# Moving half a chunk of gates ahead of the main loop, and reordering the last three chunks, in a fused recurrence and feed-forward kernel

## The chip, the cores and the metric

The kernel runs on one core of one Trainium2 chip. The metric is the device time of one execution in microseconds (us). The engines are PE (TensorE, with its weight loads listed apart as PEld), DVE (VectorE), ACT (ScalarE), POOL (GpSimd) and SP (SyncE, which here issues nearly all DMAs).

## The reference

Two residual layers with a layer norm behind each. The first is a gated recurrence over 4096 positions of two sequences, the second a feed-forward layer with binarized weights.

```python
u = x @ W_in + b_in                       # 256 -> 64
g = sigmoid(x @ W_gate + b_gate)          # 256 -> 256
h_t = tanh(h_prev @ A + u_t @ Bm)         # one step of the recurrence
y_t = h_t @ C.T + u_t @ D.T
y_t = g_t * y_t + (1 - g_t) * x_t
x1 = layernorm(x + (ys @ W_out + b_out + x))
bw1, bw2 = alpha1 * sign(w1), alpha2 * sign(w2)
h = gelu(x1 @ bw1.T + b1)                 # 256 -> 1024
out = layernorm(x1 + h @ bw2.T + b2)
```

## The kernel before

The 4096 positions of each sequence are cut into 64 segments of 64, which run side by side, so that a recurrence step is one product of 128 x 128 states (two sequences by 64 segments). Each segment but the first starts from a guess: 48 warm-up steps over the last 48 positions come before the 64 real ones, 112 steps in all. At the end a comparison (`compare`, `count`) tells whether the guesses held; a slow path, which does not run here, stands behind it.

The rest of the work is cut into 16 chunks of 512 tokens: 4 recurrence steps times 128 columns. A chunk c goes through these parts:

- gates (`gates`, L313 on PE, tanh on ACT at L365): two halves m, each of two k products, each cut into four quarters of 128 columns. The generator takes up to `size` quarters at a time between yields. Its PSUM tiles come from the pool p_1, three buffers with the tag "h", shared with the up products.
- `mix` (L374 on PE, L381 on DVE, a row added on POOL at L359) and `mix_end` (L386 and L389 on DVE).
- `project` (L399 on PE, L410 on DVE), `stats1` (L255 to L264 on DVE, a power on POOL at L265), `shift` (L270 on DVE), `norm` (L278 on ACT, or L280 on DVE).
- a transposition of the normed chunk: `turn` does it on PE (L430), splits it on ACT (L438) and DVE (L440) and serves chunks 0, 1 and 15; `blocks` does it with a DVE transpose (L449) and sixteen DMAs on SP (L455), followed by `split_hi` (L463 on ACT) and `split_lo` (L467 on DVE), for the chunks between.
- `rest` adds a bias row on POOL (L359).
- `up` in four groups (L486 on PE, eight matmuls of 512 columns; gelu at L496 and a cast at L505 on ACT), `low` (L512 on DVE), and `down` in four groups (sixteen matmuls, L528 on PE).
- `scale` (L544) and `add` (L550) on DVE, `stats`, and `store`, which norms on ACT (L278) and writes the output (L565).

The order of all instructions is written out by hand, and each engine works through its own in that order. A function `emit` counts an assumed PE time of every piece (`COST`), and issues one recurrence step (`steps`: L157 on PE, then tanh on ACT at L158) each time the count passes `pace`. Before the loop the gates of chunks 4 to 7, 0 to 3, 8 and 9 run as small parts of three quarters between the steps (`parts`). In the loop the count is switched off, each iteration c has four places for a step, and the steps run out after iteration 10. The iteration interleaves up of chunk c, down of chunks c-1 and c, mix and project of chunk c+2 and the transposition of chunk c+1. The gates of chunks 10 to 15 come at half a chunk per iteration, from a second generator:

```python
early = gates([ch[i] for i in (4, 5, 6, 7, 0, 1, 2, 3, 8, 9)], 3)
...
late = gates(ch[10:], TB)
```

Tiles are taken from pools with a fixed number of buffers: eight for x transposed ("xt"), nine for the gates ("tg"), one each for the PSUM tags "m" (mix, project, turn) and "o" (down). DMAs wait in the order of SP's queue.

Of the kernel before, what the change touches and what calls it, by code (L numbers as in the profile page):

```python
# [18 lines left out]
KD = DM // P  # L19
# [7 lines left out]
NC = L // SPC  # L27
TB = N // P
# [9 lines left out]
def gated_recurrence_then_binary_ffn(  # L38
# [16 lines left out]
    nc = tc.nc  # L55
# [235 lines left out]
    def later(what, *args):  # L291
        if waiting is None:
            what(*args)
        else:
            waiting.append((what, args))
            if len(waiting) > 1 and not held:
                what, args = waiting.pop(0)
                what(*args)

    def gates(chunks, size, x_of=lambda c: x_tiles[c.c]):  # L300

        room = size
        for c in chunks:
            xt_ = x_of(c)
            c.t = wk.tile([P, KD, N], FP, tag="tg", name=f"tg{c.nm}", bufs=TGB)
            for m in range(KD):
                ps = p_1.tile([P, N], FP, tag="h", name=f"ps_g{c.nm}_{m}")
                for k in range(KD):
                    i = 0
                    while i < TB:  # L310
                        n = min(room, TB - i)
                        cut = bass.ds(i * P, n * P)
                        nc.tensor.matmul(  # L313
                            ps[:, cut],
                            w_gate[:, k, bass.ts(m, P)],
                            xt_[:, k, cut],
                            start=k == 0 and i == 0,
                            stop=k == KD - 1,
                            skip_group_check=True,
                        )  # L320
                        i += n
                        room -= n
                        if k == KD - 1 and i == TB:
                            later(c.tanh, m, ps)
                        if room == 0:
                            room = size
                            yield

    class Chunk:

# [28 lines left out]
                nc.gpsimd.tensor_tensor(r[:, i, :], r[:, i, :], row, ALU.add)  # L359

        def gate(self):
            yield from gates([self], TB, lambda c: c.xt)

        def tanh(self, m, ps):
            nc.scalar.activation(  # L365
# [193 lines left out]
        def store(self, blocks=range(TB), engine=nc.vector, queue=nc.sync):  # L559

            cut = slice(blocks[0], blocks[-1] + 1)
            if engine is nc.scalar:
                self.st2.shift(blocks)
            self.st2.apply(blocks, engine)
            queue.dma_start(  # L565
                out=self.at(out, self.c)[:, cut, :], in_=self.x1[:, cut, :]
            )
            yield
# [13 lines left out]
        def down_end(self):  # L582
# [28 lines left out]
            add(3)  # L611
            st2.shift([0, 1])
            store(0, nc.scalar)
            store(1, nc.scalar)
            st2.gather([2, 3])
            st2.merge([2, 3])
            st2.root([2, 3])
            store(2, nc.vector)
            store(3, nc.vector)
            yield  # L620
# [17 lines left out]
    ch = [Chunk(c, f"{c}") for c in range(NC)]  # L638
# [8 lines left out]
    def ready():  # L647
        return done < len(plan) and plan[done] // SPC in have_u

    def next_steps():  # L650
        nonlocal done
        steps(plan[done])
        done += 1
        if done == WARM:
            first_states()
        for i in range(3):
            if done == WARM + (i + 1) * SPC:
                ch[i].load_h()
        if waiting and not held:
            for what, args in waiting:  # L660
                what(*args)
            waiting.clear()

    def emit(what, pieces, pace=5600):
        nonlocal since
        for _ in pieces:
            since += COST.get(what, 0)
            if since >= pace:
                since = min(since - pace, pace // 2)
                if ready():  # L670
                    next_steps()

    def step():
        if ready():
            next_steps()

    def do(i, what, *args, pace=5600):
        if not 0 <= i < len(ch):
            return
        if what == "load":  # L680
            need = WARM + (ch[i].c + 1) * SPC
            while done < need:
                next_steps()
            ch[i].load_u()
            ch[i].load_h()
        elif what in ("load_n", "load_x", "load_gate_x"):
            getattr(ch[i], what)()
        else:
            emit(what, getattr(ch[i], what)(*args), pace)

    early = gates([ch[i] for i in (4, 5, 6, 7, 0, 1, 2, 3, 8, 9)], 3)

    def parts(n, pace):
        emit("part", (next(early, None) for _ in range(n)), pace)

    ET = mybir.EngineType
    with tc.manual_schedule(engines={ET.PE, ET.Activation, ET.DVE, ET.Pool, ET.SP}):
# [39 lines left out]
        for i in range(4):  # L737
            ch[i].xt = x_tiles[i]
        ch[0].in_x = ch[1].in_x = True
        parts(1, 600)  # L740
        do(0, "mix", pace=850)
        do(0, "mix_end")
# [13 lines left out]
        do(0, "norm")  # L756
        do(1, "project", 1, pace=1700)
        do(1, "stats1")
        parts(1, 1700)
        while waiting:  # L760
            next_steps()
        waiting = None
# [4 lines left out]
        do(1, "norm", nc.vector)  # L767
        do(0, "rest")
        next(mixed)
        parts(2, 1700)  # L770
        for i in (4, 5):
            do(i, "load_x")
        end = len(ch) - 1
        parts_met = compare()
        since = -1 << 40
        late = gates(ch[10:], TB)
        for c in range(end):
            far = 0 < c < end - 1
            if far:
                do(c + 1, "shift")  # L780
                do(c + 1, "norm")
                do(c - 1, "low", 3)
                do(c + 1, "blocks")
            do(c, "up", 0)
            if c == end - 1:
                do(c - 1, "low", 3)
                do(c + 1, "shift")
                do(c + 1, "norm")
            step()
            do(c - 1, "down", 2)  # L790
            if c > 0:
                do(c + 2, "mix")
            do(c, "low", 0)
            mixed = ch[c + 2].mix_end() if 0 < c < end - 1 else iter(())
            next(mixed, None)
            if c == end - 1:
                assert done == len(plan), done
                next(parts_met)
                next(parts_met)
            do(c + 3, "load")  # L800
            do(c + 6, "load_x")
            if c % 2 == 0:
                do(10 + c // 2, "load_gate_x")
            do(c, "up", 1)
            step()
            do(c - 1, "down", 3)
            next(mixed, None)

            if c <= 12 or c == end - 1:
                do(c - 1, "add")  # L810
            if c <= 12:
                do(c - 1, "stats")
            if 1 <= c <= 12:
                emit("gate", (next(late, None) for _ in range(KD)))
            if not far:
                do(c + 1, "turn")
            do(c, "low", 1)
            if c == end - 2:
                do(c - 1, "add")
            if c > 12:  # L820
                do(c - 1, "stats")
            if c == end - 1:
                next(parts_met)
                next(parts_met)
            do(c + 1, "rest")
            do(c, "up", 2)
            step()
            if far:
                do(c + 1, "split_hi")
            do(c, "low", 2)  # L830
            if c < end - 1:
                do(c - 1, "store", range(TB), nc.scalar)
            do(c + 3, "load_n")
            do(c, "down", 0)
            do(c + 2, "project", 0)
            if c == end - 2:
                do(c + 1, "split_lo")
            do(c + 2, "project", 1)
            if far and c < end - 2:
                do(c + 1, "split_lo")  # L840
            do(c + 2, "stats1")
            do(c, "up", 3)
            if c == end - 1:
                do(c - 1, "store", range(TB), nc.scalar)
            step()
            do(c, "down", 1)
# [82 lines left out]
```

## Time and profile before

| what | value |
|---|---|
| time, median of 3 runs | 437.67 us (437.33 to 437.82) |
| the profiled execution: its own time, its span | 437.67 us, 435.9 us |
| granted TensorE clock, mean | 0.994 |
| instructions | 6818 |
| matmuls of the gates, L313 | 208, busy 66.2 us |
| matmuls of the recurrence, L157 | 224, busy 43.8 us |
| up products, L486 | 512, busy 92.9 us (hi) and 80.1 us (lo) |
| row additions on POOL, L359 | 128, busy 107.6 us |

The span runs from the first to the last instruction of the core; the execution's own time is 1.8 us longer. Busy time is summed by engine. A matmul's row covers its fill and its drain, so that neighbouring rows overlap, and the start of one row after another says how fast PE goes. In a row of the timeline the brackets give the idle time of the engine before it and what ended it. The first 8 us wait for the first loads; from 8 to 86 us PE works on u, gates and steps; the loop runs from 86 to about 408 us; what follows is the last chunk, whose end (from 427 us) is DVE, ACT, POOL and the last stores.

### The profile page before, as it was taken

The page shows a single profiled execution, that of the slowest core. Times are in us where ns is not written, and L with a number is a line of the kernel's source. Part 1 is how long each engine was busy: PE and PEld are TensorE (multiplying, and loading weights), DVE is VectorE, ACT ScalarE, POOL GpSimd, SP SyncE. Part 2 cuts the span into 40 slices and gives each one's busy share as a digit, 9 for nine tenths or more (in the row PEclk, how much of TensorE's full clock was granted, in tenths as well). Part 3 has the DMA queues.
Part 4 walks back from the last instruction along what each step waited for, and adds up shares of the span by engine and source line. Part 5 has one row for each costly group of instructions (what it writes and reads, how often), then busy time and mean ns, then how long its engine had stood idle before and what let it go on. Part 6 is the DMA issues. An engine that isn't in the chain of part 4 may idle for free.

```text
span 435.9 us, 6818 instructions
## 1 busy us (share of the span) xinstructions
PE 425.5 (98%) x2402; PEld 344.3 (79%) x2402; DVE 332.4 (76%) x569; ACT 286.0 (66%) x480; POOL 155.8 (36%) x176
## 2 busy tenths in 40 slices
PE   8999999999999999999999999999999999999992
PEld 5665767788888879797979797978888888888982
DVE  0245937895979798888888897979797979797674
ACT  2443452486587776767677776777767585849881
POOL 1000050474143435253525443444343444533413
PEclk9999999999999999999999999999999999999997
DMA  8877713400251615152426242534233232311102
GB/s 297 300 282 261 269 36 128 163 2 0 44 174 44 217 46 178 38 186 80 144 66 192 76 144 69 166 102 124 91 107 109 58 111 60 111 36 50 48 2 102
DMA packets 31479, 51.34 MB, mean 118 GB/s; under 512 B 5328, under 2 KB 19664, under 8 KB 31440
## 3 DMA queue, kind: packets, MB, share of 16 engines
q1 hardware_dynamic: 30864, 50.48, 36.4%
q8 instruction: 21, 0.34, 0.3%
q10 hardware_dynamic: 576, 0.37, 0.3%
q14 instruction: 18, 0.15, 0.1%
HBM read 31.43 MB, written 8.39 MB: 91 GB/s over the span
## 4 chain that ended last, share of the span: by engine, by line
PE 89%; DVE 5%; ACT 2%; DMA 1%; issue 1%; POOL 1%; SPq 0%; POOLq 0%; DVEq 0%
PE ps_h L486 25%; PE ps_o L528 25%; PE ps_g L313 12%; PE ps_z L399 11%; PE ps_y L374 6%; PE ps_s L157 6%; PE ps_u L131 3%; DMA xt<-in_xT 1%; DVE hlo L512 1%; ACT xn L278 1%; POOL rs_b L265 1%; PE ps_t L430 1%; DVE bs_b L255 1%; DVE d L381 1%; ACT h L496 1%
## 5 line engine op out<-in xcount | busy, mean ns | idle before, releaser
L528 PE MATMUL ps_o<-sg,hhi 128*128 128x256 f32 x496 | 121.4, 286 | 0.0
L528 PE MATMUL ps_o<-sg,hlo 128*128 128x256 f32 x496 | 117.9, 279 | 0.1
L496 ACT ACTIVATE h<-ps_h,bias_c,al 128x512 f32<-128x512 f32 x128 | 95.5, 771 | 16.8 <-PE ps_h L486 13.0
L528 PEld LDWEIGHTS ps_o<-sg,hhi 128*128 128x128 f32 x496 | 93.5, 189 | 1.1 <-DVE o L544 0.3
L528 PEld LDWEIGHTS ps_o<-sg,hlo 128*128 128x128 f32 x496 | 93.5, 188 | 1.1 <-DVE hlo L512 0.3
L486 PE MATMUL ps_h<-xhi,sg 128*128 128x512 f32 x256 | 92.9, 444 | 0.3 <-ACT h L496 0.3
L359 POOL TENSOR_TENSOR xn<-xn,bo_r 128x256 f32<-128x256 f32 x64 | 54.7, 888 | 88.6 <-DMA xn<-in_x 78.4
L512 DVE TENSOR_TENSOR hlo<-h,hhi 128x1024 fp32r<-128x1024 f32 (+1 forms) x65 | 79.5, 1240 | 5.0 <-ACT hhi L505 5.0
L486 PE MATMUL ps_h<-xlo,sg 128*128 128x512 f32 x256 | 80.1, 394 | 0.2
L265 POOL TENSOR_TENSOR rs_b<-rs_b,neg_half 128x4 f32<-128x4 f32 (+1 forms) x17 | 28.1, 1655 | 115.1 <-DVE rs_b L264 105.0
L505 ACT CAST hhi<-h 128x1024 fp32r<-128x1024 f32 (+1 forms) x65 | 67.4, 1039 | 2.0
L313 PE MATMUL ps_g<-xt,w_gate 128*128 128x384 f32 (+3 forms) x208 | 66.2, 430 | 0.1
L486 PEld LDWEIGHTS ps_h<-xhi,sg 128*128 128x128 f32 x256 | 46.5, 189 | 18.9 <-issue 11.7
L158 ACT ACTIVATE st<-ps_s 64x128 f32<-64x128 f32 x112 | 30.0, 268 | 45.7 <-PE ps_s L157 45.3
L486 PEld LDWEIGHTS ps_h<-xlo,sg 128*128 128x128 f32 x256 | 48.0, 188 | 11.9 <-DVE xlo L440 0.7
L157 PEld LDWEIGHTS ps_s<-st,wab 128*128 128x128 f32 x224 | 38.5, 189 | 21.6 <-ACT st L158 9.7
L359 POOL TENSOR_TENSOR xn<-xn,b_r 128x256 f32<-128x256 f32 x64 | 52.9, 855 | 1.1 <-PE ps_t L430 1.1
L399 PE MATMUL ps_z<-w_out,tg 128*128 128x256 f32 x224 | 50.6, 379 | 0.0
L399 PEld LDWEIGHTS ps_z<-w_out,tg 128*128 128x128 f32 x224 | 41.4, 190 | 5.1
L157 PE MATMUL ps_s<-st,wab 128*128 128x128 f32 x224 | 43.8, 277 | 0.1
L278 ACT ACTIVATE xn<-xn,nm_a,rs_a 128x256 f32<-128x256 f32 x60 | 31.2, 591 | 14.4 <-DVE nm_a L270 14.3
L265 POOL TENSOR_TENSOR rs_a<-rs_a,neg_half 128x4 f32<-128x4 f32 x16 | 17.2, 1072 | 65.0 <-DVE rs_a L264 63.0
(79 smaller groups left out, 481.5 us busy)
## 6 DMA issues: line engine op xcount, KB each, us to landing
xt<-in_xT SPq DMA_DIRECT2D x35, 512.0 KB, 4.4
xn<-in_x SPq DMA_DIRECT2D x16, 512.0 KB, 3.4
out_y<-xn SPq DMA_DIRECT2D x15, 512.0 KB, 2.6
xlo<-xb SPq DMA_DIRECT2D x208, 32.0 KB, 1.9
hu<-st SPq DMA_DIRECT2D x32, 128.0 KB, 2.3
w1t<-in_w1T SPq DMA_DIRECT2D x2, 512.0 KB, 4.9
w1n<-in_w SPq DMA_DIRECT2D x2, 512.0 KB, 6.1
w2t<-in_w2T SPq DMA_DIRECT2D x2, 512.0 KB, 5.2
```

The lines of the kernel that those rows point to most:

```text
L157: nc.tensor.matmul(p_h, ab, st[:, j].rearrange("p b k -> p (b k)"), start=True, stop=True)
L158: nc.scalar.activation(h_of[:, j + 1].rearrange("p b k -> p (b k)"), p_h[TOP, :], AF.Tanh)
L265: nc.gpsimd.tensor_tensor(rs, rs, neg_half[:, cut], ALU.pow)
L278: nc.scalar.activation(r, r, AF.Identity, bias=self.sh[:, i : i + 1], scale=rs)
L313: nc.tensor.matmul(ps[:, cut], w_gate[:, k, bass.ts(m, P)], xt_[:, k, cut], start=k == 0 and i == 0, stop=k == KD - 1, skip_group_check=True,)
L359: nc.gpsimd.tensor_tensor(r[:, i, :], r[:, i, :], row, ALU.add)
L399: nc.tensor.matmul(self.ps_z[:, i, :], self.y[:, k, bass.ts(i, P)], w_out[:, k, :], start=k == 0, stop=k == KD - 1,)
L486: nc.tensor.matmul(ps, sg1[:, k, bass.ts(j, P)], part[:, k, :], start=n == 0, stop=n == 2 * KD - 1,)
L496: nc.scalar.activation(to, ps.rearrange("p (a i c) -> p a i c", a=P // 32, c=32) if self.far else ps, AF.Gelu, bias=b1_c[:, j : j + 1], sc ...
L505: nc.scalar.copy(hi[:, part, :], h[:, part, :])
L512: nc.vector.tensor_sub(lo[:, i, :], h[:, i, :], hi[:, i, :].bitcast(FP))
L528: nc.tensor.matmul(ps[:, i, :], part[:, j % 2, bass.ts(tb, P)], sg2[:, j, :], start=j == 0 and part is self.h[j // 2][0] and first, stop=j ...
```

## The change

- One generator `stream` now serves all gates. Its piece size is a list of one number that is changed from 3 quarters to 4 before the loop. Two more parts are taken before the loop, one before `turn` of chunk 0 and one at the loop's entrance: with them half of chunk 10's gates (one m of two) is done there. The load of chunk 10's x for the gates moves ahead of chunk 0's mix; in the loop the gates begin with iteration 2.
- The step that stood behind the first up group of an iteration now stands behind the first down group (chunk c-1's third). Iteration 0, which has no such down group, issues no step there.
- In iteration 13, `rest` of chunk 14 and the store of chunk 12 move behind project and stats1 of chunk 15, the store behind the last up group. The store's shift on DVE is taken out of it and put behind `split_lo` of chunk 14; `store` skips the shift where it has been done.
- In iteration 14, `turn` and `rest` of chunk 15 move from before to behind the third up group of chunk 14.

No arithmetic is added or removed.

```diff
     def gates(chunks, size, x_of=lambda c: x_tiles[c.c]):
 
-        room = size
+        room = size[0]
...
                         if room == 0:
-                            room = size
                             yield
+                            room = size[0]
...
-            if engine is nc.scalar:
+            if engine is nc.scalar and not hasattr(self.st2, "sh"):
                 self.st2.shift(blocks)
...
-    early = gates([ch[i] for i in (4, 5, 6, 7, 0, 1, 2, 3, 8, 9)], 3)
+    size = [3]
+    stream = gates([ch[i] for i in (4, 5, 6, 7, 0, 1, 2, 3, 8, 9, *range(10, NC))], size)
...
+        do(10, "load_gate_x")
         parts(1, 600)
         do(0, "mix", pace=850)
...
         do(1, "stats1")
-        parts(1, 1700)
+        parts(2, 1700)
         while waiting:
             next_steps()
...
         next(mixed)
-        parts(2, 1700)
+        parts(3, 1700)
...
-        late = gates(ch[10:], TB)
+        size[0] = TB
...
-            step()
             do(c - 1, "down", 2)
+            if c > 0:
+                step()
             if c > 0:
                 do(c + 2, "mix")
...
-            if c % 2 == 0:
+            if c > 0 and c % 2 == 0:
                 do(10 + c // 2, "load_gate_x")
...
-            if 1 <= c <= 12:
-                emit("gate", (next(late, None) for _ in range(KD)))
-            if not far:
+            if 2 <= c <= 12:
+                emit("gate", (next(stream) for _ in range(KD)))
+            if c == 0:
                 do(c + 1, "turn")
...
-            do(c + 1, "rest")
+            if c < end - 2:
+                do(c + 1, "rest")
             do(c, "up", 2)
+            if c == end - 1:
+                do(c + 1, "turn")
+                do(c + 1, "rest")
             step()
...
-            if c < end - 1:
+            if c < end - 2:
                 do(c - 1, "store", range(TB), nc.scalar)
...
             if c == end - 2:
                 do(c + 1, "split_lo")
+                ch[c - 1].st2.shift(range(TB))
             do(c + 2, "project", 1)
...
             do(c + 2, "stats1")
+            if c == end - 2:
+                do(c + 1, "rest")
             do(c, "up", 3)
-            if c == end - 1:
+            if c >= end - 2:
                 do(c - 1, "store", range(TB), nc.scalar)
```

More of the change, by code (lines that the diff above doesn't have):

```diff
@@ L361, in gate @@
         def gate(self):
-            yield from gates([self], TB, lambda c: c.xt)
+            yield from gates([self], [TB], lambda c: c.xt)
         def tanh(self, m, ps):
@@ L689, in do @@
             emit(what, getattr(ch[i], what)(*args), pace)
-    early = gates([ch[i] for i in (4, 5, 6, 7, 0, 1, 2, 3, 8, 9)], 3)
+    size = [3]
+    stream = gates([ch[i] for i in (4, 5, 6, 7, 0, 1, 2, 3, 8, 9, *range(10, NC))], size)
     def parts(n, pace):
-        emit("part", (next(early, None) for _ in range(n)), pace)
+        emit("part", (next(stream) for _ in range(n)), pace)
     ET = mybir.EngineType
```

## The prediction

> **What bounds the kernel now.** I read the page first, then the windows by stage, then the chain of waits in order of time, then the timeline of each engine around the places where the chain leaves PE.
>
> ```profile
> PE 425.5 (98%) x2402; PEld 344.3 (79%) x2402; DVE 332.4 (76%) x569; ACT 286.0 (66%) x480; POOL 155.8 (36%) x176
> ...
> PE 89%; DVE 5%; ACT 2%; DMA 1%; issue 1%; POOL 1%; SPq 0%; POOLq 0%; DVEq 0%
> ```
>
> PE is the bound, and no other engine is near it. But a PE row includes its pipelined end, so 98% busy hides short stalls. The windows (PE busy first after the length) say where to look:
>
> ```profile
> 82.00:94.00 12.00, 11.67 (x62) 8.87 (x60) 11.24 (x20) 10.09 (x18) 8.85 (x10) 1.00 0.13 47
> 94.00:380.00 286.00, 286.00 (x1626) 239.54 (x1625) 238.93 (x404) 207.62 (x323) 118.86 (x128) 1.00 0.35 104
> 380.00:410.00 30.00, 29.65 (x185) 25.85 (x184) 26.58 (x51) 22.85 (x31) 10.43 (x9) 1.00 0.12 34
> ```
>
> From 94 to 380 us PE never stops, at granted clock 1.00: there, only moving work to or from PE counts. Gaps lie at the loop's entrance and in chunks 13 and 14. PE's timeline shows them:
>
> ```profile
> 83.25 0.52 PE L430 MATMUL ps_t<-ident,xn 128*128 128x128 f32 x3
> 83.93 0.77 PE L430 MATMUL ps_t<-ident,xn 128*128 128x128 f32 x5 [0.17 <-ACT xn L278]
> 84.53 0.60 PE L239 MATMUL ps_al<-al,ones 128*128 128x256 f32 x2
> ...
> 85.98 0.70 PE L486 MATMUL ps_h<-xhi,sg 128*128 128x512 f32 x2
> 86.59 1.10 PE L486 MATMUL ps_h<-xlo,sg 128*128 128x512 f32 x2
> ...
> 90.74 0.49 PE L157 MATMUL ps_s<-st,wab 128*128 128x128 f32 x2
> ...
> 391.85 0.62 PE L486 MATMUL ps_h<-xhi,sg 128*128 128x512 f32 x2
> 392.54 0.74 PE L486 MATMUL ps_h<-xlo,sg 128*128 128x512 f32 x2
> 393.57 0.73 PE L486 MATMUL ps_h<-xhi,sg 128*128 128x512 f32 x2 [0.28 <-ACT h L496]
> ```
>
> Compare starts, not durations. Chunk 0's turn takes 1.28 us from 83.25 to 84.53, where chunk 1's takes 0.80 to 0.87 (91.06 to 91.86). Chunk 14's first up group takes 2.75 us (391.85 to the first down product at 394.60), where the chain gives 1.83 for eight such matmuls. ACT and DVE tell why chunk 14 is late:
>
> ```profile
> 389.21 1.05 ACT L463 CAST xhi<-xlo 128x1024 fp32r<-128x1024 f32 x1 [4.48 <-DVE hlo L512]
> 390.77 2.08 ACT L278 ACTIVATE xn<-xn,nm_b,rs_b 128x256 f32<-128x256 f32 x4 [0.51 <-DVE nm_b L270]
> 392.75 1.43 ACT L496 ACTIVATE h<-ps_h,bias_c,al 128x512 f32<-128x512 f32 x2
> ...
> 390.03 0.70 DVE L270 SCALAR_TENSOR_TENSOR nm_b<-mv_b,rs_b 128x4 f32<-128x4 f32 x1 [0.91 <-POOL rs_b L265]
> 390.78 1.71 DVE L467 TENSOR_TENSOR xlo<-xlo,xhi 128x1024 fp32r<-128x1024 f32 x1
> ```
>
> ACT puts chunk 12's store (L278) ahead of the last gelus of chunk 13 (L496), whose PSUM tile up(14,0) needs; DVE puts that store's shift, which waits for POOL's power, ahead of split_lo(14) (L467).
>
> **The change part by part.** The sum is made against the profiled execution, 437.67 us for a span of 435.9; 437.67 is also the median of the runs shown.
>
> **1. Half of chunk 10's gates before the loop.** Counting room by quarters (128 columns, 0.645 us per three, so 0.215 each): 54 parts covered 160 quarters, 56 parts cover 168. Eight quarters, 1.72 us, enter before the loop; chunk 1 loses two 512-column pairs, also 1.72 (112.93 to 114.65 in the chain). PE's total is unchanged; what can change is stalls. Before, from step 67 (82.38) to down(0,0) (93.92) is 11.54 us. Content: 5 steps at 0.22 (1.10), 7 quarters (1.51), two turns at 0.87 (1.74), mean_w2 0.44, three up groups at 1.83 (5.49): 10.28. Stalls: 1.26. With the change, the same content plus 1.72:
> - Part 53 and step 68 now come before turn(0), and reach it at 84.1. The wait for the norm ending at 83.88 is covered, but step 68 itself wants to start at 83.89 and needs step 67's tanh, which ACT does behind the norm and ends at 84.04: new stall 0.2.
> - Three parts and step 69 after mean_w2 put up(0,0) at 87.8 instead of 85.98. Its low halves (DVE L440) end at 87.13: that wait goes, and so does the one of the step at 90.74, now issued early.
> - ACT starts chunk 0's gelus 1.1 us later, so step 71 (wants 94.29) meets step 70's tanh (about 94.26): 0.05, up to 0.2.
> Down(0,0) comes at 82.38 + 12.0 + 0.25 = 94.6, 0.7 later than before; chunk 1 gives 1.72 back. Gross gain 1.0.
>
> The extra tanh of chunk 10 (0.67 us) moves on ACT from 114.69 to about 88, between hi(0) and the first gelu, which PE doesn't offer before 88.7: nothing. Its load of 512 KB (4.4 us) moves on SP ahead of chunk 1's states; its buffer was free once the u of chunks 13 to 15 or chunk 8's gates were done (64 us), and SP issues nothing between 63.7 and 67.25: nothing. If SP did wait for longer, chunk 1's states (issued 67.25, landed 69.76) would hold mix(1), at 70.67, by all beyond 0.9 us.
>
> **What covers chunk 1 then?** The price is here: the half of the gates also hid the block transposes of chunk 2.
>
> ```profile
> 121.45 1.05 ACT L463 CAST xhi<-xlo 128x1024 fp32r<-128x1024 f32 x1 [2.89 <-DMA xlo<-xb]
> 122.40 2.08 ACT L278 ACTIVATE xn<-xn,nm_b,rs_b 128x256 f32<-128x256 f32 x4
> 124.39 1.42 ACT L496 ACTIVATE h<-ps_h,bias_c,al 128x512 f32<-128x512 f32 x2
> ```
>
> The sixteen DMAs land at 121.4 whatever PE does. up(2,0) moves from 125.90 to 124.18: hi is ready at 122.5, lo (DVE L467) at about 123.8 and wanted at 124.64, but its second half wants at 125.1 the PSUM tile that the gelu starting at 124.39 frees at 125.2 (the same pair freed PE 0.82 after its start at 393.57). New stall 0.1, and about 0.1 more where the next step meets ACT. Net of part 1: 0.8.
>
> **2. The step behind the first down run.** The step keeps its two 109 ns matmuls and its 0.27 us tanh. Without the move, chunk 2's step would stand at 126.1 and wait for the tanh at 126.79 to 127.05; moved, it stands at 127.9. That saves 0.9 us that part 1 would otherwise cost, and nothing against before. On ACT the tanh stays behind the cast, which ends 2 us after the moved step: no blocking. The trace has no step between a down run and a mix; its four places cost 0.28 (the moved one), 0.15, 0.18 and 0.21 us, as differences of the chain between iterations 5 and 11, the one with steps and the other without. Ten steps move, so the new place may give 0.1 each or take 0.03. Part of the 0.28 is a slower pace of down matmuls (117 against 113 ns each), which no step sets, so I take 0 and keep -1.0 to +0.3 in all.
>
> **3. Chunk 13's order.** split_lo(14) can follow split_hi (ends 390.26): done at 391.5, not 392.5. up(14,0)'s lo is wanted at 392.3: 0.24 gone. The gelus of up(13,3) start at 390.2 instead of 392.75, freeing their tile at 391.0, wanted at 392.77: the rest of the 0.92 gone. The store then runs 392.6 to 394.7 and gelu(14,0) ends at 396.0 against 396.6: no new wait. rest(14) (four POOL adds, 3.80 us) now starts after POOL's power for chunk 15, near 396.8. Here a rule speaks against the change: with it beside split_lo, L467 took 1.71 us, beside none 1.23 (123.17): 0.48 per instruction. The Trainium skill, "SBUF — State Buffer", section "Who interferes with whom", says that a DVE instruction with two SBUF inputs and a GpSimd one that reads SBUF exclude each other fully. By the row, low(14,0), add(13) and low(14,1), now beside the adds, lose 0.5 each; by the rule up to one add each, 0.95. lo(15) then ends at 407.1 or 408.2; wanted at about 408.0. By the row nothing, by the rule 0.2 lost. The measured row stands for this pair: nothing.
>
> **4. Turn 15.** After part 3 PE reaches the old place of turn(15) at 399.2, and norm(15) ends there too (ACT: cast to 397.1, then 2.08): it would stall 0.2 to 0.4. Behind up(14,2) it stands at 401.05. up(14,2) now wants at 400.1 the tile of gelu(14,1), free at 399.9: 0 to 0.2, I take 0.05. hi(15) goes behind two gelus and a cast on ACT, 404.0 to 405.0; lo(15) 405.5 to 406.7; up(15,0) at 407.6: covered by 0.9. rest(15) is behind the turn on POOL and needed only at the end. The tail (9 us of the last chunk) moves along whole. Parts 3 and 4: 0.92 - 0.05, and 0.1 of the count's wait (408.22 to 408.43), makes 0.9.
>
> Sum: 0.8 + 0 + 0.9 = 1.7, less 0.1 for small waits that I can't see: 1.6. **437.67 - 1.6 = 436.1 us.**
>
> **Rivals.**
> - *A wait takes half of it.* One end gives nothing: ACT, with 10.09 of 12 us busy around the entrance, or the tile of up(14,2). Then 0.8 or 0.9 stays: 436.8. For it: I found margins of 0.05 to 0.2 us in three places. Against: each such miss costs a tenth or two, not the whole.
> - *The lost cover of chunk 2's blocks (slower).* The DMAs take 13.4 us from first issue to last landing in chunk 1, against 11.0 to 13.0 later. If PE's new order makes the norm or the DMAs later, each us goes straight into up(2,0) since the margin there is below zero. 1.6 us later is even with before; beyond 2.5 it is slower by over 0.2%. At 3.0 the time is 437.67 + 1.4 = 439.1. Against: DVE waited 1.29 us for PE before x1(2), so the chain starts from PE and moves with it.
> - *It only moves stalls (same).* All of part 1 and half of part 3 returns as the same waits one group later: 437.3. Against: PE's stalls had named owners, and those are out of the way.
>
> **How the numbers follow.** Forecast 0.65, range of its own 435.4 (all stalls gone, no new ones: 1.26 + 0.92 + 0.1 = 2.3) to 436.7; half of it 0.14; only moved 0.10; slower by the lost cover 0.11. About 0.2%, 0.9 us, is what a measurement of this kernel can tell from no change (the edge is 436.8): faster 0.72 (the forecast and half of the second case), same 0.16, slower 0.12. The range, 435.4 to 437.3, leaves out the slower case and little else.
>
> **What would show it.** Right: PE from 82 to 94 fully busy but for 0.2 us at a step near 84; up(0,0) near 87.8; up(2,0) about 0.8 us earlier than before; up(14,0) taking 1.9 us; L467 of chunk 14 at 1.2 us and ahead of L270; turn(15) without a wait. Wrong: gaps before L486 of chunk 2 named after xlo or a gelu, a wait of SP between 63 and 68 us that delays mix(1), or PE's content growing between 94 and 380.

## The result: 1.0 us faster, and where the profile after shows it

| kernel | median | lowest to highest | executions | ratio to before, 95% interval |
|---|---|---|---|---|
| before | 437.92 us | 437.33 to 438.61 | 9 | 1 |
| after | 436.78 us | 436.24 to 438.51 | 9 | 0.9978 (0.9968 to 0.9987) |

The ratio is a gain of 0.22%, 1.0 us (0.6 to 1.4); the two medians stand 1.1 us apart. The forecast was 436.1, in a range of 435.4 to 437.3. Against the 437.67 of the profiled execution, on which the sum was built, the median of after stands 0.9 us lower, where 1.6 was forecast: the direction is right, and the sum is too large by some 0.7 us. One execution of after in a later group took 621.59 us at a granted clock of 0.655, and the ratios leave it out.

The profiled execution of after took 438.51 us, the longest of its nine, since it began late: step 67 of the recurrence, the last piece ahead of everything the change touches but the order of one load, starts at 83.73 us instead of 82.38, and the chain of waits names a first load of the gate weights. Times of different traces are therefore counted from the start of step 67 here. The windows of after, moved by the same 1.35 us (length, then busy time of PE, PEld, DVE, ACT and POOL, granted clock, DMA share, GB/s):

```profile
83.35:95.35 12.00, 11.98 (x65) 9.75 (x64) 10.25 (x20) 9.70 (x17) 8.11 (x9) 1.00 0.01 2
95.35:381.35 286.00, 286.00 (x1629) 239.86 (x1628) 239.86 (x402) 207.95 (x324) 122.85 (x129) 1.00 0.35 104
381.35:411.35 30.00, 29.91 (x186) 26.18 (x186) 27.44 (x52) 22.66 (x32) 12.43 (x10) 1.00 0.11 33
```

The entrance is full (11.98 of 12.00, before 11.67), and the last stage nearly so. The page's busy times:

```profile
PE 426.7 (98%) x2406; PEld 346.5 (79%) x2406; DVE 332.9 (76%) x569; ACT 285.3 (65%) x480; POOL 159.7 (37%) x176
```

PE's busy share is the same 98%: a change of 1 us in 437 can't be read there. It is read from starts. PE's timeline at the entrance of the loop:

```profile
83.95 1.46 PE L313 MATMUL ps_g<-xt,w_gate 128*128 128x384 f32 x4
85.43 0.49 PE L157 MATMUL ps_s<-st,wab 128*128 128x128 f32 x2
85.76 1.04 PE L430 MATMUL ps_t<-ident,xn 128*128 128x128 f32 x8
86.63 0.60 PE L239 MATMUL ps_al<-al,ones 128*128 128x256 f32 x2
...
88.95 0.91 PE L486 MATMUL ps_h<-xhi,sg 128*128 128x512 f32 x2
```

Chunk 0's turn now takes 0.87 us (85.76 to 86.63) instead of 1.28, and up(0,0) starts 5.22 us after step 67. Step 68 is the row at 85.43. It starts 1.48 us after the gates ahead of it, which take 1.30 where nothing waits behind them (in the first kernel of the third group below): 0.18 us of waiting for step 67's tanh, which ACT ends at 85.37.

At the other end, ACT and DVE around chunk 14:

```profile
390.33 1.05 ACT L463 CAST xhi<-xlo 128x1024 fp32r<-128x1024 f32 x1 [4.75 <-DVE hlo L512]
391.28 1.44 ACT L496 ACTIVATE h<-ps_h,bias_c,al 128x512 f32<-128x512 f32 x2
392.76 1.05 ACT L505 CAST hhi<-h 128x1024 fp32r<-128x1024 f32 x1
393.71 2.07 ACT L278 ACTIVATE xn<-xn,nm_b,rs_b 128x256 f32<-128x256 f32 x4
395.69 1.43 ACT L496 ACTIVATE h<-ps_h,bias_c,al 128x512 f32<-128x512 f32 x2
...
391.41 1.22 DVE L467 TENSOR_TENSOR xlo<-xlo,xhi 128x1024 fp32r<-128x1024 f32 x1 [1.26 <-ACT xhi L463]
392.55 0.15 DVE L270 SCALAR_TENSOR_TENSOR nm_b<-mv_b,rs_b 128x4 f32<-128x4 f32 x1
```

The gelus of chunk 13 (L496 at 391.28) now run ahead of chunk 12's store (L278), and split_lo (L467) runs ahead of the store's shift (L270) in 1.22 us instead of 1.71. The chain of waits in order of time shows what came of it, and what came instead:

```profile
382.56 1.15 DVE o L544
383.71 0.04 issue
383.75 2.10 PE ps_o L528 x16
385.86 3.45 PE ps_z L399 x16
389.31 1.85 PE ps_h L486 x8
391.16 1.89 PE ps_o L528 x16
393.04 1.86 PE ps_h L486 x8
394.91 1.84 PE ps_o L528 x16
396.74 1.83 PE ps_h L486 x8
398.58 1.83 PE ps_o L528 x16
400.41 2.11 PE ps_h L486 x8
402.52 0.87 PE ps_t L430 x8
```

up(14,0), at 393.04, takes 1.86 us, before 2.75. But up(14,2), at 400.41, takes 2.11 instead of 1.83, and at 383.75 down(13,0) follows DVE's scale (L544), not PE's own work. PE starts, in us after step 67, from three traces of the same kernel after (the two later ones are runs described below):

| start of | before | after | after, again | after, third |
|---|---|---|---|---|
| up(0,0) | 3.59 | 5.22 | 5.22 | 5.22 |
| up(1,0) | 20.84 | 21.73 | 21.67 | 21.77 |
| up(2,0) | 43.35 | 42.65 | 42.56 | 42.69 |
| up(3,0) | 65.86 | 65.30 | 65.27 | 65.36 |
| up(14,0) | 309.47 | 309.15 | 309.03 | 309.10 |
| up(15,0) | 326.16 | 325.30 | 325.11 | 325.36 |
| last down run (chain) | 343.47 | 342.61 | 342.44 | 342.67 |

The gain at the last product is 0.86, 1.03 and 0.80 us. It is made in two places, 0.50 to 0.59 by up(3,0) and 0.43 to 0.61 between up(14,0) and up(15,0); 0.13 to 0.24 is lost on the way to up(14,0).

### The profile page after: what moved, and what is told of

The parts are those of the page before. It is cut to its first block, busy times and chain, and to the rows that moved or that the text cites. A ratio compares the mean times of both kernels' runs of the same rounds, so it can differ in the third digit from the quotient of the medians.

```text
span 436.6 us, 6829 instructions
## 1 busy us (share of the span) xinstructions
PE 426.7 (98%) x2406; PEld 346.5 (79%) x2406; DVE 332.9 (76%) x569; ACT 285.3 (65%) x480; POOL 159.7 (37%) x176
## 4 chain that ended last, share of the span: by engine, by line
PE 87%; DVE 4%; SPq 2%; ACT 2%; DMA 2%; issue 1%; POOL 1%; POOLq 0%; DVEq 0%
PE ps_h L486 24%; PE ps_o L528 23%; PE ps_g L313 13%; PE ps_z L399 12%; PE ps_s L157 6%; PE ps_y L374 6%; PE ps_u L131 3%; SPq L455 2%; DMA w_gate<-in_W_gate 1%; ACT xn L278 1%; DVE hlo L512 1%; DVE xlo L467 1%; DVE bs_a L255 1%; PE ps_t L430 1%; DMA hu<-st 1%
## 5 line engine op out<-in xcount | busy, mean ns | idle before, releaser
L496 ACT ACTIVATE h<-ps_h,bias_c,al 128x512 f32<-128x512 f32 x128 | 95.2, 770 | 15.0 <-PE ps_h L486 11.5
L359 POOL TENSOR_TENSOR xn<-xn,bo_r 128x256 f32<-128x256 f32 x64 | 58.1, 941 | 89.7 <-DMA xn<-in_x 84.1
L512 DVE TENSOR_TENSOR hlo<-h,hhi 128x1024 fp32r<-128x1024 f32 (+1 forms) x65 | 78.6, 1227 | 4.8 <-ACT hhi L505 4.6
L313 PE MATMUL ps_g<-xt,w_gate 128*128 128x384 f32 (+3 forms) x212 | 67.5, 432 | 0.3 <-DMA w_gate<-in_W_gate 0.3
L265 POOL TENSOR_TENSOR rs_b<-rs_b,neg_half 128x4 f32<-128x4 f32 (+1 forms) x17 | 28.1, 1655 | 107.0 <-DVE rs_b L264 102.0
L157 PEld LDWEIGHTS ps_s<-st,wab 128*128 128x128 f32 x224 | 38.2, 191 | 21.5 <-ACT st L158 10.4
L265 POOL TENSOR_TENSOR rs_a<-rs_a,neg_half 128x4 f32<-128x4 f32 x16 | 17.1, 1070 | 68.3 <-DVE rs_a L264 68.3
L278 ACT ACTIVATE xn<-xn,nm_a,rs_a 128x256 f32<-128x256 f32 x60 | 31.2, 590 | 16.1 <-DVE nm_a L270 16.1
```

The source lines that it names most:

```text
L157: nc.tensor.matmul(p_h, ab, st[:, j].rearrange("p b k -> p (b k)"), start=True, stop=True)
L265: nc.gpsimd.tensor_tensor(rs, rs, neg_half[:, cut], ALU.pow)
L278: nc.scalar.activation(r, r, AF.Identity, bias=self.sh[:, i : i + 1], scale=rs)
L313: nc.tensor.matmul(ps[:, cut], w_gate[:, k, bass.ts(m, P)], xt_[:, k, cut], start=k == 0 and i == 0, stop=k == KD - 1, skip_group_check=True,)
L496: nc.scalar.activation(to, ps.rearrange("p (a i c) -> p a i c", a=P // 32, c=32) if self.far else ps, AF.Gelu, bias=b1_c[:, j : j + 1], sc ...
L512: nc.vector.tensor_sub(lo[:, i, :], h[:, i, :], hi[:, i, :].bitcast(FP))
```

## The experiments

The experiments take the terms of the sum one by one; "part 1" to "part 4" are those of the prediction. Every kernel was timed in five rounds, and the kernels of one group ran on one chip.

### First group: halves and parts

**Part 1 alone, the step where it was.** The end of after is undone, and the step stands ahead of the down run:

```diff
             do(c, "up", 0)
...
+            if c > 0:
+                step()
             do(c - 1, "down", 2)
-            if c > 0:
-                step()
```

> Part 1 alone: half of chunk 10's gates before the loop, the step behind the first up group as before, the end as before. If the moved step is what keeps part 1's gain (prediction, part 2), chunk 2's step waits for the tanh behind chunk 1's last cast: 0.9 us of PE gap ahead of down(1,2), so the entrance's gain of 0.6 to 0.7 us goes and the kernel is 0.1 to 0.4 us slower than before (ratio 1.000 to 1.001). Rival, that the moved step only costs time in ten iterations: this is the better half of the change, 0.6 to 0.9 us faster than before (ratio 0.998).

Measured: 437.82 us, ratio 1.0002 (0.9994 to 1.0010), before beside it 437.88. PE's timeline in chunk 2 has the stall that the prediction derived for the step's old place:

```profile
127.38 0.49 PE L157 MATMUL ps_s<-st,wab 128*128 128x128 f32 x2 [0.40 <-ACT st L158]
```

The stall is 0.40 us, where the prediction derived 0.9. Part 1 alone is worth nothing that can be measured. In its trace up(2,0) comes 0.85 us earlier than before, but chunk 2 then takes 23.13 us instead of 22.51, and up(3,0) comes only 0.23 earlier.

**Parts 1 and 2, the entrance complete.** After, with its end as before.

> Parts 1 and 2, the end as before. The prediction gives 0.8 us. Aligned on step 67, the changed kernel's trace gives 0.70 by the start of chunk 1's project and 0.56 by chunk 2's: the theory from the trace is 0.5 to 0.6 us faster than before (ratio 0.9987). Rival, that stalls only move: within 0.2 us of before.

Measured: 437.22 us, ratio 0.9988 (0.9979 to 0.9996). In its trace up(3,0) comes 0.62 us earlier than before, and the last stage is that of before (16.69 us from up(14,0) to up(15,0) in both). The step's move is worth 437.82 - 437.22 = 0.6 us inside part 1 by the medians, whose intervals just touch, and 0.39 by the starts of up(3,0).

**Parts 3 and 4, the end alone.** Before, with the hunks of iterations 13 and 14.

> Parts 3 and 4 alone, entrance and steps as before. The prediction's sum gives 0.9 us faster (ratio 0.998). Theory from the changed kernel's trace: 0.9 gained at up(14,0), but 0.28 lost at up(14,2), whose second half waits for the PSUM tile of gelu(14,1), which stands behind norm(15) on ACT, and 0.1 to 0.2 in the pace and the waits around it: 0.4 to 0.5 us faster (ratio 0.999).

Measured: 437.56 us, ratio 0.9993 (0.9985 to 1.0001), so 0.3 us, not separated from nothing. In its profiled execution the end gained nothing at all, 17.09 us from up(14,0) to up(15,0) against 16.69; PE's timeline says why:

```profile
392.33 0.74 PE L486 MATMUL ps_h<-xlo,sg 128*128 128x512 f32 x2 [0.20 <-DVE xlo L467]
...
400.96 0.73 PE L486 MATMUL ps_h<-xhi,sg 128*128 128x512 f32 x2 [0.55 <-ACT h L496]
```

Chunk 14's block DMAs landed 307.67 us after step 67 in this trace, where before has 306.57 and after 306.35. Most of the reason lies on SP: from the first of the sixteen issues to the last it took 10.53 us here, 9.93 in before and 9.71 in after, and the last one landed 1.86 to 1.87 us behind its issue in all three. hi(14) is late by that, and then everything behind it on ACT; the wait shows at split_lo's product and again at the third up group's tile. Why SP issued more slowly is open, and so is whether it did in the executions without a profile.

**Part 2 alone.** Before, with the step moved behind the down run and left out of iteration 0.

> Part 2 alone in the kernel before: the step behind the first down run, none of it in iteration 0 (the last steps run one iteration later). Theory: no PE gap hung on it, so 0.1 us either way (ratio 0.9998 to 1.0002); the period of iterations 3 to 9 stays 22.51 us. Rival, that the step costs less between down and mix than between up and down: 0.5 to 1.0 us faster and a period of 22.4; rival on the other side: a period of 22.55 and 0.3 slower.

Measured: 438.11 us, ratio 1.0007 (1.0000 to 1.0013), which is 0.3 us slower. From iteration 3 to 9 the period is 22.51 us with the step at the old place and at the new one: the place itself costs nothing. What the trace loses, it loses elsewhere. The step of iteration 0 ran in a gap ahead of chunk 1's turn. Without it PE reaches the turn early and waits inside it for DVE's norm (L280), and up(1,0) comes no earlier (20.92 us after step 67, before 20.84):

```profile
90.60 1.52 PE L430 MATMUL ps_t<-ident,xn 128*128 128x128 f32 x8
```

Before, that row took 1.04 us; by the starts the turn takes 1.28 us instead of 0.79. The step itself comes back in iteration 11, which takes 21.88 us from up(11,0) to up(12,0) instead of 21.69. The profiled execution (438.56 us) loses 0.28 more in chunk 14, where the block DMAs landed as late as in the end alone (307.85 us after step 67).

### Second group: which edit of the end pays

**After, once more**, as the neighbour of this group.

> The changed kernel once more, beside its variants. Theory from the first runs: the entrance gives 0.5 us, the end 0.3, so 0.8 us faster than before (ratio 0.998). From step 67 to the end of the span 352.9 us, as in its first trace, give or take 0.4 for the landing of chunk 14's block DMAs.

Measured: 436.65 us, ratio 0.9971 (0.9961 to 0.9980), before beside it 437.83.

**Turn 15 at its old place.** This undoes part 4 alone:

```diff
             if not far:
                 do(c + 1, "turn")
...
+            if c == end - 1:
+                do(c + 1, "rest")
             do(c, "up", 2)
-            if c == end - 1:
-                do(c + 1, "turn")
-                do(c + 1, "rest")
             step()
```

> The changed kernel with turn and rest of chunk 15 at their old place, before the third up group of chunk 14. The prediction (part 4): turn stands at norm(15)'s end and waits, 0.2 to 0.4 us slower than the changed kernel. Theory from the traces: norm(15) ends 0.9 us after PE gets there, less the stall of up(14,2) that this order hides (0.3): 0.3 to 0.6 us slower than the changed kernel (ratio to before 0.999). Rival, that the move only traded one wait for another: equal to the changed kernel.

Measured: 436.39 us, ratio 0.9966 (0.9954 to 0.9979): not slower than after; the intervals overlap. The prediction had a stall of 0.2 to 0.4 us here. PE's and ACT's timelines:

```profile
398.60 1.12 PE L430 MATMUL ps_t<-ident,xn 128*128 128x128 f32 x8
...
396.82 2.08 ACT L278 ACTIVATE xn<-xn,nm_a,rs_a 128x256 f32<-128x256 f32 x4 [0.33 <-DVE nm_a L270]
```

The norm begins at 396.82 and ends at 398.90, 0.30 after the turn has begun, and PE's row names no wait. The norm is four instructions of about 0.5 us, a block each, and the turn's eight matmuls read block by block, 0.11 us each: by 398.60 three blocks are there, and the fourth comes while PE transposes the first ones. By the starts the turn takes 0.88 us instead of 0.79, a stall of 0.1. And with the turn between them, up(14,2) comes later and finds its tile free: it shows no wait. From up(14,0) to up(15,0) this kernel takes 15.88 us, after again 16.08.

**rest(14) at its old place**, POOL's four adds beside split_lo(14).

> The changed kernel with rest of chunk 14 (four POOL additions) at its old place, beside split_lo of chunk 14. If DVE and POOL exclude each other, L467 of chunk 14 takes 1.7 instead of 1.22 us and PE waits up to 0.4 us in up(14,0); nm_a of chunk 15 (0.70 beside POOL) gets its 0.16 back. Theory: 0.0 to 0.4 us slower than the changed kernel. Rival, that the place of rest is all that part 3 is: 0.9 slower.

Measured: 436.88 us, ratio 0.9976 (0.9967 to 0.9985), beside after's 436.65 unclear. DVE's row:

```profile
389.69 1.66 DVE L467 TENSOR_TENSOR xlo<-xlo,xhi 128x1024 fp32r<-128x1024 f32 x1 [1.01 <-ACT xhi L463]
```

The adds cost split_lo 0.44 us (1.66 against 1.22), and up(14,0) goes without a wait all the same: what part 3 gained there is the order of the gelus and of split_lo, not the place of rest. But the place shows at up(14,2), whose tile comes late by 0.50 us (2.34 us by the starts instead of 1.84), more than in any trace of after. The adds delay DVE, the shift of chunk 15 comes later, and ACT waits for it 0.75 us ahead of norm(15), where after waits 0.32.

**norm(15) behind up(14,1), turn and rest 15 behind down(14,0).** This takes the 2.08 us of norm(15) out of ACT's way to gelu(14,1), which frees that tile.

> The changed kernel with norm(15) emitted behind up(14,1) instead of before it, and turn(15) and rest(15) behind down(14,0). ACT then does gelu(14,1) before the norm, so the PSUM tile that up(14,2) waits for is free 2 us earlier. Theory: the stall in up(14,2) (0.16 + 0.12 us in the first trace, 0.83 in the end-only kernel) goes, turn doesn't wait: 0.3 us faster than the changed kernel (ratio to before 0.9973 to 0.9977). Rival, that hi and lo of chunk 15 come too late: a wait in front of up(15,0), equal or 0.3 slower.

Measured: 436.80 us, ratio 0.9972 (0.9961 to 0.9982), as after. The stall of up(14,2) is gone, and a new one stands behind it. DVE's timeline:

```profile
397.84 0.83 DVE L166 TENSOR_TENSOR d<-st 64x126 f32<-64x126 f32 x1
398.71 0.72 DVE L168 TENSOR_TENSOR d<-d 64x126 f32<-64x126 f32 x1
399.35 1.21 DVE L544 TENSOR_TENSOR o<-ps_o,al_r 128x1024 f32<-128x1024 f32 x1
```

down(14,0) needs the PSUM tile that scale(13) (L544) reads, done at 400.56; at its pace PE would have been there at 400.44. The compare of the guesses (L166, L168) stands ahead of it, and beside rest(14) on POOL (396.02 to 400.04) its two rows take 0.83 and 0.72 instead of 0.28 each in before.

### Third group: a better version

**After, a third time.**

> The changed kernel a third time, as the reference of the two variants beside it: 0.9 to 1.2 us faster than before (ratio 0.9973 to 0.998), with its stalls in up(14,2) of 0.16 to 0.2 us and 0.2 at step 68.

Measured: 436.59 us, ratio 0.9961 (0.9947 to 0.9974), before beside it 438.29.

**The old turn, and no step among the two parts ahead of turn(0).** Its second edit lets PE do both parts first, so that step 68 comes later, when its tanh is long done:

```diff
-        parts(2, 1700)
+        parts(2, 1 << 30)
         while waiting:
             next_steps()
```

> The changed kernel with turn(15) and rest(15) at their old place, and no step between parts 53 and 54 (steps 68 and 69 come behind parts 54 and 56). Theory: PE no longer meets step 67's tanh behind the norm (0.2 us), nor the tile of gelu(14,1) (0.3 us): 0.4 to 0.5 us faster than the changed kernel, ratio to before 0.996 to 0.997; from step 67 to up(0,0) 5.0 instead of 5.22 us. Rival for the entrance: turn(1) then waits for chunk 1's norm on DVE, and the 0.2 us comes back as that wait.

Measured: 435.99 us (435.85 to 436.78), ratio 0.9955 (0.9942 to 0.9969), the lowest median of all kernels; 0.6 us below after beside it, with intervals that overlap. The two edits were not run apart. PE's timeline, to be held against that of after above:

```profile
82.81 1.46 PE L313 MATMUL ps_g<-xt,w_gate 128*128 128x384 f32 x4
84.11 1.04 PE L430 MATMUL ps_t<-ident,xn 128*128 128x128 f32 x8
...
87.73 0.70 PE L486 MATMUL ps_h<-xhi,sg 128*128 128x512 f32 x2
```

The turn follows the gates with nothing between. up(0,0) starts 5.14 us after step 67 (after 5.22), up(1,0) 21.41 (21.77), the last product 341.61 (342.67). From up(14,0) to up(15,0) it takes 15.79 us (after beside it 16.26). The new stalls at step 68 and up(14,2) are gone from this profile; chunk 2 still takes 22.66 us.

**Store and split_lo reordered, nothing else at the end**: rest(14), turn(15) and rest(15) at their old places.

> Of the end's order only the store of chunk 12 moved (its shift behind split_lo(14), its norm behind up(13,3)); rest(14), turn(15) and rest(15) stand where they stood before. Theory: the store is all that the end gains by; L467 takes 1.66 us again, which PE feels only when the block DMAs land late; 0.1 to 0.4 us faster than the changed kernel. Rival, that rest beside split_lo costs a wait in up(14,0): equal to the changed kernel or slower.

Measured: 436.96 us, ratio 0.9967 (0.9956 to 0.9979), 0.4 us above after beside it, not separated. In its profile the turn at the old place does wait:

```profile
399.95 0.33 PE L430 MATMUL ps_t<-ident,xn 128*128 128x128 f32 x1 [0.16 <-ACT xn L278]
```

By the starts the turn takes 1.17 us instead of 0.79, a stall of 0.38. Two delays meet here: the block DMAs landed 2.62 us ahead of up(14,0) (2.87 and 2.97 in the two kernels above that have the old turn and no such stall), and rest(14) stands beside split_lo as in the kernel with a wait of 0.75 for the shift. The stall that the prediction named for the old turn exists, in the size named, when norm(15) is late. It isn't there by itself.

## Why the prediction was right, and where its sum failed

**Right in kind.** PE is the bound, its stalls at the entrance and in chunk 14 had named causes, and both edits remove these causes: up(0,0) at 5.22 us after step 67 (foretold 5.4), down(0,0) 0.77 us later than before (foretold 0.7), step 68's wait of 0.2, up(14,0) in 1.86 us (foretold 1.9), L467 at 1.22 us ahead of L270. The slower rival, block DMAs that are too late for up(2,0), has nothing for it: the cast there starts 39.58 us after step 67, split_lo ends at 42.28, and up(2,0) begins at 42.65, without a wait.

**Part 1, 0.8 foretold, 0.50 to 0.59 measured.** Its gross gain was put at 1.0, 1.72 given back less 0.7. Chunk 1 gives back 1.59 (22.51 to 20.92 from up(1,0) to up(2,0)), and up(1,0) is 0.83 to 0.93 late, not 0.7. No wait stands there. A little of it is PE's pace: a down run of sixteen goes at about 114.2 or at 117.8 ns for each matmul, which is 0.06 us a run. Of the down runs between up(1,0) and up(2,0), two went at 114.1 in before and go at 117.8 in every trace of after, and one went at 117.8 and goes at 114.3 to 114.5.

The next step of the prediction failed in its working: it put up(2,0) at 124.18, which is before's 125.90 in the chain (125.73 by its start) less the whole 1.72, though the 0.7 lost at the entrance comes first. On before's clock, up(2,0) came at 82.38 + 42.65 = 125.03. Of the two waits of 0.1 each that it drew from this, the one for a gelu's PSUM tile in up(2,0) isn't in any trace. The one where a step meets ACT is there, one step later: chunk 2 takes 0.14 us more (22.65 against 22.51), and the step behind its second up group starts at 133.91, just behind the tanh that ACT ends at 133.86. Nor do the DMAs "land at 121.4 whatever PE does": the cast that waits for them starts 0.5 us later (39.58 us after step 67, before 39.07).

**Part 2, 0 foretold, 0 measured, with the right condition.** The period of an iteration doesn't change, and part 1 without it is worth nothing (1.0002). The saving of 0.9 inside part 1 was 0.4 to 0.6. One reading behind the 0 was wrong: the prediction held that no step sets the slower pace of down matmuls. The step's place decides which run has it. In the three kernels with the step ahead of a chunk's third down run (before and two variants), that run goes at 117.8 ns in 7 to 9 of chunks 1 to 9 and the fourth in none; in the ten profiles with the step behind it, the fourth goes at 117.8 in 8 or 9 and the third in at most one. The slow run moved and did not go away, so the 0 held, in part by luck; why a run is slow stays open. That the step dropped from iteration 0 had filled a gap was not in the prediction; with part 1 the gap is filled by gates.

**Parts 3 and 4, 0.9 foretold, 0.43 to 0.61 measured: here is the mis-sized term.** up(14,0) gave 0.88 of its 0.92. The term that failed is the 0.05 us for up(14,2)'s tile, in part 4. It had the right place and the right cause (gelu(14,1)) and an end of 0.2 for its range; the traces have 0.28, 0.29 and 0.47 us for after, where the block DMAs landed 2.80, 2.80 and 2.62 us ahead of up(14,0), and 0.83 in the end alone, where they landed 1.78 ahead. From hi(14) to gelu(14,1) ACT works without a pause but for the 0.32 that norm(15) waits for its shift:

```profile
398.52 2.08 ACT L278 ACTIVATE xn<-xn,nm_a,rs_a 128x256 f32<-128x256 f32 x4 [0.32 <-DVE nm_a L270]
400.51 1.43 ACT L496 ACTIVATE h<-ps_h,bias_c,al 128x512 f32<-128x512 f32 x2
```

So a late landing reaches PE undiminished, or nearly: in the end alone, 1.0 us later than in after, it costs 0.47 at up(14,0) and 0.55 more at up(14,2). The 0.32 itself is what the sum left out. The sum let norm(15) follow the cast at once; but its shift (L270) waits for the power on POOL that stands just ahead of rest(14), starts 0.06 us behind the first add of rest and takes 0.70 us instead of 0.15:

```profile
397.79 0.70 DVE L270 SCALAR_TENSOR_TENSOR nm_a<-mv_a,rs_a 128x4 f32<-128x4 f32 x1 [0.90 <-POOL rs_a L265]
398.41 1.21 DVE L512 TENSOR_TENSOR hlo<-h,hhi 128x1024 fp32r<-128x1024 f32 x1
...
397.73 3.99 POOL L359 TENSOR_TENSOR xn<-xn,b_r 128x256 f32<-128x256 f32 x4
```

Without the 0.32 the tile would be free at 400.95 instead of 401.27, and PE wants it at 401.17: the whole wait of the first trace. In the two later traces the same sum clears the wait too, in the third by 0.02 us. That is worked out from the starts; no run here puts rest(14) behind that shift. PE's rows, in the first profile of after, name no wait; it is read from the starts:

```profile
400.70 0.62 PE L486 MATMUL ps_h<-xlo,sg 128*128 128x512 f32 x2
401.32 0.74 PE L486 MATMUL ps_h<-xhi,sg 128*128 128x512 f32 x2
401.90 0.62 PE L486 MATMUL ps_h<-xlo,sg 128*128 128x512 f32 x2
```

From 400.70 to 401.90 it takes 1.20 us, where the pace of 0.46 gives 0.92. Turn(15) at its old place fills that time with transposes, which is why the kernel without part 4 loses nothing. Its old place was costed against the end of the whole norm (399.2), though the turn needs it block by block, and PE reaches the last block 0.33 us after the first.

The other terms: the 0.1 of the count's wait doesn't come (the count's matmul at 408.91 starts 0.20 us behind the last one of down(14,3), before 0.21), and 0.13 to 0.24 was lost between up(3,0) and up(14,0), which was in no term. The chain of the first profile puts it at down(13,0), behind DVE's scale; but the five other kernels of the second and third group, whose order is that of after for nearly all of this stretch, take 243.54 to 243.75 us for it, before 243.61, after 243.74 to 243.85. It is scatter as much as cost. Together: 0.55 at the entrance, 0.88 less some 0.35 at the end, less 0.2 between, is 0.9, what the traces and the medians show.

**The rule that was weighed.** By the Trainium skill's "SBUF — State Buffer", "Who interferes with whom", a DVE instruction with two SBUF inputs and a POOL one that reads SBUF exclude each other. The prediction held this against a row that lost 0.48 us, and let the row decide. The two are the same: an add takes 0.74 us alone (0.95 was the mean of a row with one add held up), and the instruction loses what is left of the add that runs when it starts, less 0.13 us. In that row 0.62 us were left. In chunk 13, low starts 0.74 us before POOL's adds end at 380.35, and loses 0.61, 1.82 us instead of 1.21:

```profile
379.61 1.82 DVE L512 TENSOR_TENSOR hlo<-h,hhi 128x1024 fp32r<-128x1024 f32 x1
...
377.49 2.86 POOL L359 TENSOR_TENSOR xn<-xn,bo_r 128x256 f32<-128x256 f32 x4 [2.65 <-DMA xn<-in_x]
```

Over the thirteen profiles, 558 DVE instructions with two SBUF inputs (of seven lines) start beside an add with more than 0.16 us left, and 538 of them lose this to within 0.03 us; the other 20 lose nothing, beside an add that is itself held up. Of 368 with one SBUF input (of five lines), none loses more than 0.02. So the prediction costed the wrong instructions: low(14,0), low(14,1) and add(13) took 1.21 to 1.22 us and lost nothing, since no add had more than 0.06 us left when they started (it was the add behind low(14,1) that waited, 1.80 us instead of 0.74). The shift of chunk 15 lost 0.55, and it stands on the way to up(14,2). lo(15), where both readings had put the cost, never became late.

**The first rival was nearly the result.** "A wait takes half of it", 436.8, named the tile of up(14,2) and had a chance of 0.14; the median is 436.78, just outside the forecast's own 435.4 to 436.7. But its reason, one whole end that gives nothing, isn't what happened: the entrance gave about two thirds of its term and the end over half.

## What to carry to other kernels

When a stall on an in-order engine is taken away, follow PE to the next two tiles that it needs and compare each with the engine that frees them; here ACT had no slack left, and a third of the end's gain came back two groups later. When work on POOL moves, look at the smallest DVE instruction that now starts beside it: what it loses is the rest of the add, whatever its own size, and here it stood on ACT's path. A consumer that reads block by block waits for the block, not for the producer's end: cost a move against the first block that is late. And when a change is worth 0.2%, count from a fixed instruction inside each trace and look at several traces of the same kernel, since the start alone can differ by more than the change.

## What the hardware showed that was not expected

- The start of step 67 differed by 1.37 us between traces of one kernel (82.36 to 83.73); nearly all of it was there at step 1 (6.68 to 8.01), behind the first loads. The stretch from the last product to the end of the span differed by 0.4 us (10.0 to 10.4 for after), most of it behind DVE's last instruction, where the last stores land (median 2.4 to 2.7 us after their issue).
- What a DVE instruction loses beside POOL's adds does not depend on its own size: L166 goes from 0.28 to 0.82 us, the shift L270 from 0.15 to 0.70, split_lo from 1.22 to 1.66, each by the rest of one add less 0.13. POOL loses by the same count: the power L265 takes 1.02 us alone and 1.86 when it starts 0.98 us before a low on DVE ends.
- A run of down matmuls has two paces, about 114.2 and 117.8 ns each, at a granted clock of 1.00. At the entrance the same run of one program can have either (the second of chunk 0 has 117.8 and 114.2 in two traces of after); in the loop it goes with the run's place in PE's order, as part 2 above showed. The fourth run of a chunk in after has 117.8 with POOL busy beside it and with POOL idle.
